# Two-layer graph convolution: the second layer's first 16 tiles gather before the last 212 hidden rows are stored, and small last groups share gather buffers

## The chip, the cores and the metric

The kernel runs on one core of one Trainium2 chip. The metric is the device time of one execution in microseconds (us); the time before is the median of 14 runs. The core has five engines with a queue each: TensorE (PE, with its weight loads as PEld), VectorE (DVE), ScalarE (ACT), GpSimd (POOL) and SyncE (SP). Every queue runs in its order, and semaphores tie the queues together. POOL issues all gathers here, SP nearly all other transfers.

## What is computed

There are N = 12500 nodes with 128 channels and E = 200000 edges, sorted by destination. Each edge has one of 10 relations, the argmax over 10 of its attribute columns. A layer averages the source rows of each (destination, relation), applies that relation's weights, and adds a root product and a bias. Two such layers, the first with a relu, are followed by a residual and a layer norm:

```
sums = segment_sum(x[src], dst * 10 + edge_type)
mean = sums / max(count, 1)
layer(x) = einsum('nrd,rdo->no', mean, w_rel) + x @ root + bias
h   = relu(layer1(x))
out = layernorm(x + layer2(h))
```

Layer 2 gathers rows of h, so in general it needs all of h.

## The kernel before

**Tiles and groups.** The edges are cut into NT = 1563 tiles of 128. A group is G = 16 tiles; NS = 95 full groups (0 to 94, tiles 0 to 1519) are followed by the small groups that start at tiles 1520, 1528, 1536, 1544 (8, 8, 8 and 8 tiles), 1552, 1556 (4 each) and 1560 (3). Both layers run the same loop, `layer` (L532), over the groups.

**One group.** `gather` (L479) issues one indirect transfer a tile on POOL (L481): 128 rows of `x` or of the hidden table `hD`, picked by `idxE`, land in a buffer `g` of 16 tiles. Every group, a small one too, takes one of three such buffers (`RING`). `ones` (L490) makes on DVE, for each tile, a 128 x 120 matrix that has the edge's weight 1/count (`wE`) at its key (relation and offset of the destination within the tile: 10 x 12 columns) and 0 elsewhere (L496); two buffers of 16. `sums` (L500) multiplies: per tile one product g^T x oh, 128 x 120, into PSUM (L507). A full group's first product waits for all its gathers; the tiles run from last to first, and only the last product tells other engines. In the small groups each product tells by itself. PSUM holds one full group, so a group's products need DVE's adds of the group before. `add` (L519) loads the tiles' first nodes into DVE registers and adds each tile's result into the ring `circle` (L530).

**Blocks.** Nodes are finished in 29 blocks: 0 to 22 of 512 nodes, then 128 each, and block 28 of 84. `done_after` says after which tile a block is complete. Blocks 24 to 28 (from node 11904) finish among the small groups: 24 after group 94, 25 after tile 1528, 26 (nodes 12160 to 12287) after 1544, 27 (12288 to 12415) after 1556 and 28 (12416 to 12499) at the end. `projected` (L404) is a root product (L408) and ten products with the ring (L416), in two halves; ACT clears the ring after each half (L417), and DVE's later adds wait for that. `block_rows` (L428) applies bias and relu (ACT, L432) and transposes on PE (L435). In layer 1 `hidden` (L442) stores h transposed (`hT`, L447), copies the rows (ACT, L450) and stores them to `hD` (SP, L383); `block_in` (L387) loads the next block and transposes it (L400, L401). In layer 2 `final` (L453) adds the residual, normalises and stores the output.

**Order.** The queues are filled by a scheduler that keeps each engine's order by program position and readiness. In the program, group k's `ones`, gathers and products come first, then `add` of group k-1 with the blocks that it completes, then some steps of a list `todo` (L595). That list prepares edge data during layer 1: chunks of 128 tiles, one every 8 groups, each in some dozen steps (sources, types with argmax, counts with one-hot compares and PE sums, L353 to L357). Each entry has a group by which it should be done, two groups ahead of its use; the due group and the number of steps left say how many are done after each group. Among the small groups the order changes: all held adds first, `ones` one group ahead, and the add directly behind the products.

**The change of layer.** Layer 2's first gather (POOL) waits for all stores to `hD`. In layer 2, before the small groups, a flag is read by the engines (L558) that says whether a slower general path, in the `If` at L740, has to run; on these inputs it does not run.

Of the kernel before, what the change touches and what calls it, by code (L numbers as in the profile page):

```python
# [9 lines left out]
F32 = mybir.dt.float32  # L10
BF16 = mybir.dt.bfloat16
I32 = mybir.dt.int32
# [32 lines left out]
def rgcn_resnorm_kernel(ctx: ExitStack, tc: tile.TileContext, x, src, dst, attr, w_rel1, root1, b1,  # L45
# [34 lines left out]
    def done_after(k):  # L80
# [6 lines left out]
            return NT  # L87
        return min(a + n for a, n in groups if a + n >= t)

    HALF = NT * P - E  # L90
    STEP = P * N // E
    assert STEP * E == P * N and C == P and E % GT == 0 and 0 < HALF < P and NT % CT and 1 < groups[-1][1] <= G
# [27 lines left out]
    idxE = keep.tile([P, NCH * CT], I32, name="idxE")  # L120
    keyE = keep.tile([P, NCH * CT], F32, name="keyE")
    wE = keep.tile([P, NCH * CT], F32, name="wE")

    def chunk_rows(c):
        return min(CT, NT - c * CT)
# [312 lines left out]
    def spans(k):  # L438
        n = block(k)[1]
        return [(p, slice(a, b)) for p, a, b in ((P, 0, n // P), (n % P, n // P, -(-n // P))) if p and b > a]  # L440

    def hidden(k, ready, sums_of):  # L442

        xb, fT = ready
        n0, n, _ = block(k)
        a, pr = block_rows(sums_of(fT, k, 0), k, 0)
        then("SP", nc.sync.dma_start(hT[:, n0:n0 + n], a[:, :n]))  # L447
        hb = fin.tile([P, 4, C], F32, name="hb")
        for p, s in spans(k):
            nc.scalar.activation(hb[:p, s], pr[:p, s], AF.Copy)  # L450
        rows_dma(hb, hD, k, True)
# [24 lines left out]

    HELD = "clamped to a node on the chip"

    def gather(table, t0, n):  # L479
        g = gpool.tile([P, G, C], F32, name="g")  # L480
        return g, [then("POOL", nc.gpsimd.indirect_dma_start(  # L481
            out=g[:, j, :], out_offset=None, in_=table, in_offset=bass.IndirectOffsetOnAxis(
                ap=idxE[:, t0 + j:t0 + j + 1], axis=0))) for j in range(n)]

    whole = mybir.DependencyInfo(mybir.DependencyClass.Sync, mybir.DependencyReason.DATA)

    def tile_sums(zp, j):
        return zp[j // HT][:, j % HT // QB, j % QB * KW:(j % QB + 1) * KW]

    def ones(k):  # L490

        t0, n = groups[k]
        oh = dpool.tile([P, G, KW], F32, name="oh")
        for j in range(n):
            t = t0 + j
            then("DVE", nc.vector.tensor_scalar(oh[:, j, :], iotaP[:, :KW], keyE[:, t:t + 1], wE[:, t:t + 1],  # L496
                                                op0=ALU.is_equal, op1=ALU.mult))
        return oh

    def sums(table, k, oh):  # L500

        t0, n = groups[k]
        end = k >= NS
        g, gathers = gather(table, t0, n)
        zp = [ps_z.tile([P, HT // QB, YB], F32, name="zp") for _ in range(0, n, HT)]
        for j in range(n) if end else reversed(range(n)):
            m = nc.tensor.matmul(tile_sums(zp, j), g[:, j, :], oh[:, j, :], start=True, stop=True)  # L507
            then("PE", m)
            if end:
                continue  # L510
            if j < n - 1:
                tc.keep_in_program_order(m)
                continue

            for d in gathers[:j]:
                tc.add_manual_dep(m.ins, d.ins.name, whole, reason="one wait per group")
        return k, zp
# [14 lines left out]
    def layer(table, l, finish, steps, flag_too=False):  # L532
# [14 lines left out]
        for k in range(NG):  # L547
            end = k >= NS
            if k and not given and done < NBLK - 1:
                given = block_in(done, l)  # L550
            if end:

                while held:
                    add_oldest()
                if not ready:
                    ready = block_in(NBLK - 1, l)
                    if flag_too:
                        loads, (flag,) = nc.values_load_multi_w_load_instructions(  # L558
                            flag_i[0:1, 0:1], min_val=0, max_val=1, skip_runtime_bounds_check_because=HELD)
                        for ld in loads:  # L560
                            tc.keep_in_program_order(ld)
                        loaded.update(("POOL", "DVE", "PE", "ACT", "SP"))
            held.append(sums(table, k, made or ones(k)))
            made = ones(k + 1) if end and k < NG - 1 else None
# [13 lines left out]
    def chain(*gens):  # L578
        for s in gens:
            yield from s  # L580
# [14 lines left out]
    todo = []  # L595
    for c in range(1, NCH):
        s = [as_steps(sources, c + 1)] if c + 1 < NCH else []
        todo.append((c * CT // G - 2, [8 + L // DB + 2], chain(*s, types(c), count(c))))
    layer(x, 0, hidden, todo)
    def flagged():  # L600

# [14 lines left out]
    fast.close()  # L616


    gp = ctx.enter_context(tc.tile_pool(name="gp", bufs=2))
    gps = ctx.enter_context(tc.tile_pool(name="gps", bufs=1, space=PSUM))  # L620

# [153 lines left out]
```

## Time and profile before

| quantity | value |
|---|---|
| median of 14 runs | 4688.63 us (4676.69 to 4694.55) |
| profiled execution | 4688.05 us, its span 4686.3 us |
| POOL busy | 2956.3 us, 63% (3126 gathers of 0.945 us) |
| DVE busy | 1909.6 us, 41% |
| PE busy | 1868.6 us, 40% |
| ACT busy | 323.6 us, 7% |
| full groups 1 to 94 of layer 1, up to tile 1520 | 84.3 to 2314.1 us |
| small groups of layer 1 and change of layer | 2314.1 to 2411.6 us |
| full groups of layer 2 | 2411.6 to 4585.4 us |
| small groups of layer 2 and end | 4585.4 to 4686.3 us |
| granted TensorE clock | 0.667 mean |

The timeline gives for each instruction its start, its duration, the engine, the line, what it writes and reads, and in brackets how long the engine had been idle before it and what ended that idle time. "remote" and "another core or an unknown queue" stand where no releaser is found; there is only one core here. "issue" means that the engine waited for nothing that the profile shows. PE's ends are modelled from the size of an instruction, so a product's result can come later than its row says. An fp32 product is two passes, so it appears twice in the count of L507.

### The profile page before, as it was taken

The numbers are of one execution on the slowest core, as the hardware profiler recorded it, in microseconds if no ns is written. First come the engines' busy times: TensorE is split into PE (matmuls) and PEld (weight loads), VectorE is DVE, ScalarE is ACT, GpSimd is POOL, SyncE is SP. The second block draws the span as 40 slices with busy tenths as digits, with TensorE's granted clock in tenths as the row PEclk, the third lists the DMA queues.
The fourth block names the chain that finished last, engine by engine and source line by source line (L and its number), as shares of the span: only waits on it lengthen the run. The fifth ranks groups of instructions, "written<-read, shape, count | busy, mean of one in ns | idle before, by whom it ended". The sixth has DMA issues, their size and how long they took to land.

```text
span 4686.3 us, 32313 instructions
## 1 busy us (share of the span) xinstructions
PE 1868.6 (40%) x8122; PEld 1447.8 (31%) x8122; DVE 1909.6 (41%) x7125; ACT 323.6 (7%) x325; POOL 2956.3 (63%) x3136
## 2 busy tenths in 40 slices
PE   2444433344443444444532433433343343334335
PEld 1333322233232332322432333322233233223224
DVE  4344444343444434444423333333333333333344
ACT  1000010000100001000110100000000000000001
POOL 6566666666656666566656666666666666666664
PEclk7666666666666666666665766666666666666667
DMA  4222222122221222211211221222222122211221
GB/s 136 60 66 77 65 67 79 50 78 62 67 78 50 79 62 67 59 50 52 54 52 45 53 60 53 53 57 55 54 53 60 53 54 57 55 51 52 56 56 43
DMA packets 177383, 284.67 MB, mean 61 GB/s; under 512 B 57799, under 2 KB 118159, under 8 KB 174063
## 3 DMA queue, kind: packets, MB, share of 16 engines
q0 software_dynamic: 100032, 205.07, 16.6%
q1 hardware_dynamic: 73967, 77.43, 5.2%
q10 hardware_dynamic: 3190, 0.02, 0.1%
q8 instruction: 69, 1.13, 0.1%
q14 instruction: 125, 1.02, 0.1%
HBM read 262.29 MB, written 20.00 MB: 60 GB/s over the span
## 4 chain that ended last, share of the span: by engine, by line
another core or an unknown queue 39%; DVE 19%; issue 15%; PE 8%; ACT 1%; DVEq 1%; ACTq 1%
DVE acc L530 10%; DVE oh L496 7%; PE zp L507 4%; PE pp L416 2%; PE pp L408 1%; DVEq L524 1%; ACT acc L417 1%; ACTq L450 1%; DVE o L472 0%; DVE st L465 0%; PE pf L355 0%; DVE v L462 0%; ACT a L432 0%; PE pf L357 0%
## 5 line engine op out<-in xcount | busy, mean ns | idle before, releaser
L507 PE MATMUL zp<-oh,g 128*128 128x120 f32 x6252 | 1212.3, 371 | 2174.3 <-issue 1935.3
L481 POOL DMA_INDIRECT g<-in_x_dram,idxE x1563 | 1478.2, 946 | 906.1 <-issue 439.9
L481 POOL DMA_INDIRECT g<-hD,idxE x1563 | 1476.8, 945 | 795.6 <-issue 444.6
L507 PEld LDWEIGHTS zp<-oh,g 128*128 128x128 f32 x6252 | 1136.6, 279 | 2321.7 <-issue 2128.5
L530 DVE TENSOR_TENSOR acc<-acc,zp 128x120 f32 x3126 | 837.9, 268 | 2367.0 <-remote 1705.1
L496 DVE TENSOR_SCALAR oh<-bank,keyE,wE 128x120 f32<-128x120 f32 x3126 | 1196.7, 393 | 12.7 <-PE zp L507 7.0
L416 PE MATMUL pp<-acc,w 128*128 128x512 f32 (+2 forms) x1160 | 451.4, 548 | 28.4 <-DVE acc L530 19.8
L417 ACT ACTIVATE acc<-zero 128x2560 f32<-128x2560 f32 (+2 forms) x116 | 228.1, 1994 | 2539.0 <-remote 1777.0
L416 PEld LDWEIGHTS pp<-acc,w 128*128 128x128 f32 x1160 | 214.1, 208 | 231.7 <-issue 203.0
L355 PE MATMUL pf<-eqb,identb 128*128 128x512 bf16 (+2 forms) x130 | 64.7, 498 | 200.2 <-DVE eqb L353 144.6
L408 PE MATMUL pp<-fT,root 128*128 128x512 f32 (+1 forms) x112 | 76.3, 774 | 94.7 <-ACT fT L401 89.6
L353 DVE TENSOR_TENSOR eqb<-pf,kh 128x1344 bf16<-128x1344 f32 (+2 forms) x65 | 100.1, 1548 | 11.8 <-issue 7.6
L462 DVE TENSOR_TENSOR v<-pf,xb 128x512 f32<-128x512 f32 (+1 forms) x28 | 17.4, 620 | 202.5 <-remote 168.8
L357 PEld LDWEIGHTS <-identb 128*128 128x128 bf16 (+2 forms) x130 | 15.9, 122 | 224.0 <-issue 219.2
L412 ACT ACTIVATE acc<-zero 128x120 f32<-128x120 f32 x24 | 7.3, 302 | 1069.4 <-DVE acc L411 474.4
L400 PE MATMUL pf<-ident,xb 128*128 128x128 f32 x97 | 24.5, 394 | 117.5 <-ACT hb L450 105.6
L435 PE MATMUL pf<-ident,a 128*128 128x128 f32 x196 | 43.3, 352 | 60.1 <-ACT a L432 52.5
L357 PE MATMUL pf<-eqb,identb 128*128 128x512 bf16 (+2 forms) x130 | 65.7, 505 | 0.0
L408 PEld LDWEIGHTS pp<-fT,root 128*128 128x128 f32 x112 | 24.0, 262 | 101.8 <-ACT fT L401 95.5
L400 PEld LDWEIGHTS pf<-ident,xb 128*128 128x128 f32 x97 | 17.9, 210 | 120.5 <-ACT hb L450 107.6
L435 PEld LDWEIGHTS pf<-ident,a 128*128 128x128 f32 x196 | 32.2, 187 | 67.4 <-ACT a L432 58.6
L169 DVE CAST idxE<-pf 128x128 int32<-128x128 f32 (+1 forms) x13 | 3.7, 282 | 85.1 <-PE pf L168 67.7
(89 smaller groups left out, 384.3 us busy)
## 6 DMA issues: line engine op xcount, KB each, us to landing
m<-in_edge_attr_dram SPq DMA_DIRECT2D x24, 1344.0 KB
g<-in_x_dram,idxE POOLq DMA_INDIRECT x1563
g<-hD,idxE POOLq DMA_INDIRECT x1563
xb<-in_x_dram SPq DMA_DIRECT2D x46, 256.0 KB
hT<-a SPq DMA_DIRECT2D x23, 256.0 KB
hD<-hb SPq DMA_DIRECT2D x23, 256.0 KB
fT<-hT SPq DMA_DIRECT2D x23, 256.0 KB
out_dram<-o SPq DMA_DIRECT2D x23, 256.0 KB
```

Source lines behind the costliest of these rows:

```text
L353: nc.vector.tensor_tensor(eq[:p], kp[:p, None, :R].to_broadcast([p, DB, R]), fore, op=ALU.is_equal)
L355: nc.tensor.matmul(pc[:p], identb[:p, :p], eq[:p, k:k + 4, L:], start=(d + k == 1), stop=False)
L357: nc.tensor.matmul(pc[:p], identb[:p, :p], back, start=False, stop=(d + k + 3 == L))
L408: nc.tensor.matmul(po[:, :n], rsb[l], fT[:, :n], start=True, stop=False)
L416: nc.tensor.matmul(po[:, :n], wsb[l][:, r, :], circle[:, r, o:o + n], start=False, stop=(r == NREL - 1))
L417: nc.scalar.activation(circle[:, q:q + H, o:o + n], zero[:, None, :n].to_broadcast([P, H, n]), AF.Copy)
L435: nc.tensor.transpose(pr[:h, t, :], a[:, t * P:t * P + h], ident)
L450: nc.scalar.activation(hb[:p, s], pr[:p, s], AF.Copy)
L481: return g, [then("POOL", nc.gpsimd.indirect_dma_start(out=g[:, j, :], out_offset=None, in_=table, in_offset=bass.IndirectOffsetOnAxis(ap= ...
L496: then("DVE", nc.vector.tensor_scalar(oh[:, j, :], iotaP[:, :KW], keyE[:, t:t + 1], wE[:, t:t + 1], op0=ALU.is_equal, op1=ALU.mult))
L507: m = nc.tensor.matmul(tile_sums(zp, j), g[:, j, :], oh[:, j, :], start=True, stop=True)
L530: nc.vector.tensor_tensor(s, s, z, op=ALU.add)
```

## The change

It has three parts.

First, EARLY = 12288 is the first node of block 27. Layer 2's group 0 gathers from `hD[:12288]` only, with indices clamped to 12287 (`idxH`) and with weights set to 0 where the source is a later node (`wH`). So it depends on the stores of blocks 0 to 26. The part of the later nodes, 128 and 84 rows, comes by products: `late_h` keeps these rows in SBUF when `hidden` makes them, and `late_w` is a matrix of weights from late node to (tile, key). `late_sums` adds two products of 480 columns for each of four PSUM banks, in front of the group's 16 products, which now accumulate.

Second, `head`, a new last entry of `todo` due by group 94, makes `idxH`, `wH` and `late_w` in one setup step and four steps of four tiles. For each tile DVE makes three one-hot matrices (`oh`, and `of` for either late block), and PE multiplies each `of` with `oh`; ACT copies the results out. The last chunk's entry is due at 90 instead of 94, since `late_w` takes the buffers of its attributes.

Third, `gather` takes a new buffer only when the tile number is a multiple of 16, so the groups 1520 and 1528 share one, as do 1536 and 1544, and 1552, 1556 and 1560.

```
+    EARLY = starts[NBLK - 2]
...
+        i = k - (NBLK - 2)
+        hb = late_h[:, i:i + 1] if i >= 0 and not anew else fin.tile([P, 4, C], F32, name="hb")
...
+    def is_head(table, t0):
+        return table is hD and t0 < G
+
+    def head():
+        nc.vector.tensor_scalar(idxH, idxE[:, :G], EARLY - 1, None, op0=ALU.min)
+        off = keep.tile([P, 2, G], F32, name="offH")
+        nc.vector.tensor_copy(off[:, 0], idxE[:, :G])
+        nc.vector.tensor_scalar(wH, off[:, 0], float(EARLY) - 0.5, None, op0=ALU.is_lt)
+        nc.vector.tensor_tensor(wH, wH, wE[:, :G], op=ALU.mult)
+        for i in (1, 0):
+            nc.vector.tensor_scalar(off[:, i], off[:, 0], -float(starts[NBLK - 2 + i]), None, op0=ALU.add)
+        late_w.extend(prep.tile([P, P // 2 * D], F32, name=f"m{i}") for i in range(2))
+        yield
+        for b in range(0, G, QB):
+            pm = [ps_f.tile([P, YB], F32, name="pf") for _ in range(2)]
+            for j in range(QB):
+                t = b + j
+                oh = prep.tile([P, KW], F32, name="ohH")
+                nc.vector.tensor_scalar(oh, iotaP[:, :KW], keyE[:, t:t + 1], wE[:, t:t + 1],
+                                        op0=ALU.is_equal, op1=ALU.mult)
+                for i in range(2):
+                    of = prep.tile([P, P], F32, name=f"of{i}")
+                    nc.vector.tensor_scalar(of, iotaP[:, :P], off[:, i, t:t + 1], None, op0=ALU.is_equal)
+                    nc.tensor.matmul(pm[i][:, j * KW:(j + 1) * KW], of, oh, start=True, stop=True)
+            for i in range(2):
+                nc.scalar.activation(late_w[i][:, b * KW:(b + QB) * KW], pm[i][:, :QB * KW], AF.Copy)
+            yield
+
     def gather(table, t0, n):
-        g = gpool.tile([P, G, C], F32, name="g")
+        o = t0 % G
+        if not o:
+            shared["g"] = gpool.tile([P, G, C], F32, name="g")
+        g = shared["g"][:, o:o + n]
+        ix = idxE
+        if is_head(table, t0):
+            table, ix = table[:EARLY, :], idxH
...
+    def late_sums(table, t0, banks):
+        if is_head(table, t0):
+            for b, z in enumerate(banks):
+                for i in range(2):
+                    n = block(NBLK - 2 + i)[1]
+                    nc.tensor.matmul(z[:, :QB * KW], late_h[:n, i, :], late_w[i][:n, b * QB * KW:(b + 1) * QB * KW],
+                                     start=(i == 0), stop=False)
...
+        late_sums(table, t0, [zp[b // 2][:, b % 2] for b in range(G // QB)] if n == G else ())
         for j in range(n) if end else reversed(range(n)):
-            m = nc.tensor.matmul(tile_sums(zp, j), g[:, j, :], oh[:, j, :], start=True, stop=True)
+            m = nc.tensor.matmul(tile_sums(zp, j), g[:, j, :], oh[:, j, :],
+                                 start=not is_head(table, t0), stop=not is_head(table, t0) or j % QB == 0)
...
-        todo.append((c * CT // G - 2, [8 + L // DB + 2], chain(*s, types(c), count(c))))
+        todo.append((c * CT // G - (2 if s else 6), [8 + L // DB + 2], chain(*s, types(c), count(c))))
+    todo.append((NS - 1, [G // QB + 1], head()))
```

More of the change, by code (lines that the diff above doesn't have):

```diff
@@ L122, in rgcn_resnorm_kernel @@
     wE = keep.tile([P, NCH * CT], F32, name="wE")
+    late_w = []
+    idxH = keep.tile([P, G], I32, name="idxH")
+    wH = keep.tile([P, G], F32, name="wH")
+    late_h = keep.tile([P, 2, C], F32, name="late_h")
     def chunk_rows(c):
@@ L440, in spans @@
         return [(p, slice(a, b)) for p, a, b in ((P, 0, n // P), (n % P, n // P, -(-n // P))) if p and b > a]
+    anew = []
     def hidden(k, ready, sums_of):
@@ L447, in hidden @@
         then("SP", nc.sync.dma_start(hT[:, n0:n0 + n], a[:, :n]))
-        hb = fin.tile([P, 4, C], F32, name="hb")
+        i = k - (NBLK - 2)
+        hb = late_h[:, i:i + 1] if i >= 0 and not anew else fin.tile([P, 4, C], F32, name="hb")
         for p, s in spans(k):
@@ L477, in rgcn_resnorm_kernel @@
     HELD = "clamped to a node on the chip"
-    def gather(table, t0, n):
-        g = gpool.tile([P, G, C], F32, name="g")
+    shared = {}
+    def is_head(table, t0):
[24 more added lines that the diff above has]
+            yield
+    def gather(table, t0, n):
+        o = t0 % G
[5 more added lines that the diff above has]
+            table, ix = table[:EARLY, :], idxH
         return g, [then("POOL", nc.gpsimd.indirect_dma_start(
             out=g[:, j, :], out_offset=None, in_=table, in_offset=bass.IndirectOffsetOnAxis(
-                ap=idxE[:, t0 + j:t0 + j + 1], axis=0))) for j in range(n)]
+                ap=ix[:, t0 + j:t0 + j + 1], axis=0))) for j in range(n)]
     whole = mybir.DependencyInfo(mybir.DependencyClass.Sync, mybir.DependencyReason.DATA)
@@ L488, in tile_sums, with ones @@
         return zp[j // HT][:, j % HT // QB, j % QB * KW:(j % QB + 1) * KW]
-    def ones(k):
+    def ones(k, table):
         t0, n = groups[k]
         oh = dpool.tile([P, G, KW], F32, name="oh")
+        w = wH if is_head(table, t0) else wE
         for j in range(n):
             t = t0 + j
-            then("DVE", nc.vector.tensor_scalar(oh[:, j, :], iotaP[:, :KW], keyE[:, t:t + 1], wE[:, t:t + 1],
+            then("DVE", nc.vector.tensor_scalar(oh[:, j, :], iotaP[:, :KW], keyE[:, t:t + 1], w[:, t:t + 1],
                                                 op0=ALU.is_equal, op1=ALU.mult))
         return oh
+    def late_sums(table, t0, banks):
[5 more added lines that the diff above has]
+                                     start=(i == 0), stop=False)
     def sums(table, k, oh):
@@ L562, in layer @@
                         loaded.update(("POOL", "DVE", "PE", "ACT", "SP"))
-            held.append(sums(table, k, made or ones(k)))
-            made = ones(k + 1) if end and k < NG - 1 else None
+            held.append(sums(table, k, made or ones(k, table)))
+            made = ones(k + 1, table) if end and k < NG - 1 else None
             if end or len(held) > 1:
@@ L616, in rgcn_resnorm_kernel @@
     fast.close()
+    anew.append(True)
     gp = ctx.enter_context(tc.tile_pool(name="gp", bufs=2))
```

## The prediction

> **What bounds the kernel now.** I read the page first, then the POOL, PE, DVE and ACT timelines around the change of layer and at the end, because the page is a mean over stages.
>
> ```profile
> PE 1868.6 (40%) x8122; PEld 1447.8 (31%) x8122; DVE 1909.6 (41%) x7125; ACT 323.6 (7%) x325; POOL 2956.3 (63%) x3136
> ...
> another core or an unknown queue 39%; DVE 19%; issue 15%; PE 8%; ACT 1%; DVEq 1%; ACTq 1%
> ```
>
> POOL is the busiest engine, and the largest share of the chain of waits has no named releaser. The POOL timeline shows the rhythm: one gather each 1.25 us (0.94 and a 0.30 gap), so a group of 16 is a run of 19.7 us, and then POOL waits for a buffer. These are the starts of layer 2's groups 0, 3 and 4.
>
> ```profile
> 2411.61 0.94 POOL L481 DMA_INDIRECT g<-hD,idxE  x1 [25.38 <-PE pp L408]
> ...
> 2479.10 0.94 POOL L481 DMA_INDIRECT g<-hD,idxE  x1 [7.84 <-remote]
> ...
> 2501.91 0.94 POOL L481 DMA_INDIRECT g<-hD,idxE  x1 [3.15 <-remote]
> ```
>
> The change of layer costs 25.38 us. Later groups start 22.8 us apart, a run of 19.7 and a wait of 3.1. What is that wait? PE and DVE of the same stretch:
>
> ```profile
> 2433.03 6.02 PE L507 MATMUL zp<-oh,g 128*128 128x120 f32 x32 [22.40 <-DMA g<-hD,idxE]
> 2482.81 3.74 PE L507 MATMUL zp<-oh,g 128*128 128x120 f32 x16 [43.77 <-DVE acc L530]
> ...
> 2478.93 0.28 DVE L530 TENSOR_TENSOR acc<-acc,zp 128x120 f32 x1 [66.53 <-remote]
> ...
> 2501.68 0.28 DVE L530 TENSOR_TENSOR acc<-acc,zp 128x120 f32 x1 [14.65 <-remote]
> ```
>
> Group 0's 32 passes (two per product) are entered at 2433.03 to 2439.05, yet DVE's add, which waits only for them, starts at 2478.93: 7.7 us after POOL's run of 48 gathers ended (2471.26). Group 1 repeats it: PE by 2489.8, DVE at 2501.68, 2.9 us after POOL's run ended at 2498.8. DVE itself was quiet from 2487.0. So I read: **while POOL issues gathers and DVE and ACT are quiet, PE's results come at a crawl**, (2478.9 - 2433.0) / 32 = 1.43 us a pass, where they are entered at 0.19. ACT's clearing of the ring, half a block after each five products, tests it on one shape:
>
> ```profile
> 4636.38 0.74 ACT L417 ACTIVATE acc<-zero 128x640 f32<-128x640 f32 x1 [10.86 <-PE pp L416]
> 4642.73 0.74 ACT L417 ACTIVATE acc<-zero 128x640 f32<-128x640 f32 x1 [5.62 <-remote]
> ...
> 4658.63 0.74 ACT L417 ACTIVATE acc<-zero 128x640 f32<-128x640 f32 x1 [9.52 <-PE pp L416]
> 4660.36 0.74 ACT L417 ACTIVATE acc<-zero 128x640 f32<-128x640 f32 x1 [0.99 <-PE pp L416]
> ```
>
> The same five products take 6.35 us under a run (4630.68 to 4645.4; DVE quiet from 4637.7) and 1.73 without. The cause of the crawl is not in the trace; I use it as found. [...]
>
> Last, the end of layer 1 (tiles 1520 on), where each small group takes a buffer of its own:
>
> ```profile
> 2325.75 0.94 POOL L481 DMA_INDIRECT g<-in_x_dram,idxE  x1 [1.88 <-remote]
> ...
> 2341.67 0.95 POOL L481 DMA_INDIRECT g<-in_x_dram,idxE  x1 [6.23 <-PE zp L507]
> ...
> 2354.75 4.59 PE L416 MATMUL pp<-acc,w 128*128 128x128 f32 x20 [6.89 <-DVE oh L496]
> ...
> 2363.62 1.51 ACT L417 ACTIVATE acc<-zero 128x640 f32<-128x640 f32 x2 [18.08 <-remote]
> ...
> 2391.05 0.32 SPq L383 DMA_DIRECT2D hD<-hb  x1
> ...
> 2409.04 0.33 SPq L383 DMA_DIRECT2D hD<-hb  x1
> ```
>
> POOL waits between short runs, and in these waits PE gets through. The last two lines are the stores of block 26 and of the last 84 nodes; layer 2's first gather follows the last store by 2.57 us.
>
> **The change, part by part.** Times are against the profiled execution: 4688.05 us, span 4686.3 and 1.75 around it; the median of 14 runs is 0.6 above.
>
> *Early gathers.* Group 0 of layer 2 needs block 26 (rows below 12288), not blocks 27 and 28. The stores lie 2409.04 - 2391.05 = 18.0 us apart, so its 16 gathers may move 18.0 earlier, and group 1 (20.0 after group 0) still finds the last rows landed. They pass nothing on POOL's queue; SP's stores are the same. Alone: -18.0.
>
> *Shared buffers, layer 1's end.* Tiles 1520 to 1535 become one run, 2314.08 to 2333.8, without the wait at 2325.75. But that wait let group 93's products finish (DVE had them at 2325.51). Now DVE falls quiet at about 2322 with some 12 passes left: 12 x 1.43 = 17 us, or the run's end and 2.9, so 2336.7, the ordinary rhythm: +11.2. Run B (1536 to 1551) is 2336.9 to 2356.6. Behind group 93 on PE stand block 22's projection (8.8 us), then through ACT its four transposes (about 4 at the crawl), then group 94's 32 passes, of which most stay until the run ends: about 2363, where now it is 2341.4: +21.6. DVE's adds, the six projections left and ACT queue behind it. From there to the last store the trace has 67.6 us; of these 10.2 are crawl (DVE's 5.58 us wait at 2351.61, where PE needed 1.9: 3.7; ACT at 2363.62, not 2357.1: 6.5). The last run (11 gathers, 2363.3 to 2377.0) covers fewer of them; I charge 3. Last store: 2363 + 67.6 - 10.2 + 3 = 2423.4, +14.4. Bounds: 0 (group 94 as now) and +21.6 (nothing of the crawl saved).
>
> *Sum at the change of layer.* Group 0 at 2391.05 + 14.4 + 2.57 = 2408.0, its run to 2427.7; last rows landed at 2426.0, about 1 later if the early run slows the last blocks (DVE has the next factors to make there, so little). Group 1 at 2428.6, now 2431.6: -3. Group 0 then has 8 more products of 480 columns, 16 passes at 0.43 (the 512-column rows at L416 step so) = 6.9 us if all lie after the run, 0 if they fit in it; I take 3. So 0 in all, bounds -18 and +12.
>
> *Making the late factors.* 48 DVE one-hots at 0.39 = 18.8 us, 32 products of 64 passes (13 us at 0.2), 8 ACT copies at 0.6, in four steps over layer 1's last groups. DVE is quiet 14.65 us per group, so the work itself is covered. The tiles of0, of1 and ohH have one buffer each: DVE waits for PE four times a step, and main adds stand behind it in DVE's order; POOL waits for those. Nearest rows: layer 1's groups with a finished block, three round trips between PE and ACT, start 26.8 us apart (group 88) against 22.8: +4 a step. Part of this wait falls under busy DVE, so +2.5 a step, +10. Below nothing: starts 20.0 apart occur where DVE stays busy, -2.8 a step, -11; above: 16 passes crawling, 23 us a step less the 11.4 that PE now loses under a run, +46. The last chunk's steps come earlier, four a group instead of two, onto the quiet 14.65 us: 0, bounds -3 and +8.
>
> *Shared buffers, layer 2's end.* Group 92 done 4585.1; run A to 4605.1 without the break at 4596.99; group 93 at 4607.8 (now 4596.7); group 94 between 4622 and 4632 (now 4608.5), as ACT's and DVE's final steps keep PE going or not: +19. Less the crawl now in the rest (6.35 - 1.73 = 4.6 at 4642.73; 3.7 at L462, 4647.83 after products of 4643.78), plus 3: +14 at the end. Bounds -8 and +21.
>
> Sum: 0 + 10 + 0 + 14 = +24: 4688.05 + 24 = **4712**.
>
> **Rivals.** *No price for long runs (faster).* If PE keeps pace in a run of 16 in the last groups, as it did at 4604.35 to 4608.5 under a run of 8, both ends stay where they are and the 18.0 is kept: 4670 with the factors at 0. It decides if group 93's products are done by about 2327 in the new trace. Against it: every full group of layer 2.
> *The factors stall layer 1.* If each wait of DVE for PE makes DVE quiet and PE crawls, a step costs about 9 (group 84's 30.1 against 22.8 is 7.3, the dearest late one): 4 x 6.5 more, 4738.
> *The early gathers still wait for the last rows,* if that wait is on all stores of hD: group 0 at 2426.0, group 1 at 2446.0, +14.4 instead of -3: 4729.
> *The ends cancel:* early gathers and factors as above, group 94 half as late at both ends: about 4712 - 7 - 10, or 4695, and 4688 with free factors.
>
> **How the numbers follow.** Two results within 0.2% (9.4 us) can't be told apart here. Forecast (4699 to 4725) 0.40, stalled factors 0.17, no early start 0.07: slower 0.64. Ends cancel 0.14: same. Free long runs 0.22: faster. The likeliest is 4712, own range 4699 to 4725. For 8 in 10: down to 4668, which takes in 4670 with 2 to spare and leaves 0.1 below; up to 4750, the stalled factors and half their bound.
>
> **What would show it.** Early start right: layer 2's first gather starts while the products of block 27 or 28 still run, and POOL's 25.38 us idle shrinks. Shared buffers as said: POOL's last runs are 16, 16 and 11, and DVE's first add of group 93 comes 2 to 3 us after the first of them ends; ACT's L417 and DVE's first adds say "remote" there. Factors: starts of groups 89 to 94 above 25. The forecast falls if the end groups' products are seen promptly inside the runs, or if the scheduler gives DVE other work there, which by the rows above would keep PE going.

## The result, and the profile after

The changed kernel takes 4734.25 us (median of 6 runs, 4726.69 to 4739.91) against 4688.63 before (28 runs): 1.0099 times as long, 95% interval 1.0089 to 1.0109. It is 45.6 us slower; the forecast was 23, at 4712 us. The measured time lies above the forecast's own range (4699 to 4725) and inside its wider one (4668 to 4750). The kernel before itself took 3950 us in one of the four later comparisons and 4685 to 4728 in the other three (3950 and 4686 on one and the same chip), so every kernel below is compared only with runs of the kernel before that were made beside it, and the two conditions are named by their rhythm in layer 2, groups 20.0 us apart or groups 22.7 to 23.0 apart.

The page of the changed kernel, its busy times and then the engines' shares of the chain of waits:

```profile
PE 1895.0 (40%) x8202; PEld 1467.6 (31%) x8202; DVE 1927.4 (41%) x7179; ACT 328.0 (7%) x333; POOL 2953.6 (62%) x3136
...
another core or an unknown queue 28%; DVE 14%; issue 6%; PE 2%; DVEq 1%; ACT 0%; DMA 0%; ACTq 0%
```

The work added is small (PE 26 us more, DVE 18), and POOL does the same gathers. So the loss must be in waits. POOL's timeline of the changed kernel shows where: the start of tile 1520 in layer 1, the next gather that waited, layer 2's groups 0 and 1, and then layer 2's tiles 1520, 1536 and 1552.

```profile
2310.72 0.94 POOL L529 DMA_INDIRECT g<-in_x_dram,idxE  x1 [3.26 <-remote]
...
2379.43 0.94 POOL L529 DMA_INDIRECT g<-in_x_dram,idxE  x1 [29.09 <-PE zp L566]
...
2424.02 0.94 POOL L529 DMA_INDIRECT g<-hD,idxH  x1 [31.16 <-DMA hD<-hb]
...
2451.04 0.94 POOL L529 DMA_INDIRECT g<-hD,idxE  x1 [7.36 <-PE pp L415]
...
4601.98 0.94 POOL L529 DMA_INDIRECT g<-hD,idxE  x1 [3.12 <-remote]
...
4624.69 0.94 POOL L529 DMA_INDIRECT g<-hD,idxE  x1 [3.04 <-remote]
...
4646.85 0.94 POOL L529 DMA_INDIRECT g<-hD,idxE  x1 [2.50 <-remote]
```

Tile 1520 of layer 1 starts 3.4 us earlier than before (2310.72, was 2314.08). Then 32 gathers run without a stop, where POOL waited twice before (at 2325.75 and 2341.67), and POOL stands 29.09 us for group 94. Layer 2's first gather is 12.4 us later than before (2424.02, was 2411.61), group 1 is 19.4 later (2451.04, was 2431.6), tile 1520 of layer 2 is 16.6 later (4601.98, was 4585.38). From there to the end it takes 125.3 us (4727.3 - 4601.98) where it took 100.9. So: -3 before tile 1520, some +20 at the end of layer 1 and the change of layer, +24 at the end of layer 2.

What POOL waited for at 2379.43 stands in DVE's, PE's and SP's rows of the same stretch:

```profile
2318.78 8.76 PE L423 MATMUL pp<-acc,w 128*128 128x512 f32 x20
...
2324.85 0.91 DVE L590 TENSOR_TENSOR acc<-acc,zp 128x120 f32 x3 [8.92 <-remote]
...
2358.65 1.12 PE L442 MATMUL pf<-ident,a 128*128 128x128 f32 x4 [31.12 <-ACT a L439]
...
2359.56 0.62 PE L515 MATMUL pf<-ohH,of 128*128 128x120 f32 x2
...
2361.33 0.40 DVE L510 TENSOR_SCALAR ohH<-bank,keyE,wE 128x120 f32<-128x120 f32 x1 [35.57 <-PE pf L515]
...
2372.38 6.78 PE L566 MATMUL zp<-oh,g 128*128 128x120 f32 x32 [3.33 <-DVE acc L590]
...
2421.55 0.32 SPq L390 DMA_DIRECT2D hD<-hb  x1
...
2448.81 0.33 SPq L390 DMA_DIRECT2D hD<-late_h  x1
```

Read it from the DVE row at 2361.33. DVE stood 35.57 us in front of a one-hot of the last factor step (L510), because the buffer was still held by a product (L515) that stands on PE behind block 22's projection (L423) and transposes (L442). The projection was entered by 2327.5, but PE's transposes waited 31.12 us for ACT, which waited for the projection to be seen (ACT cleared the ring's first half at 2343.76, the second at 2355.69); POOL's run of gathers ended at 2350.34. DVE's later adds and one-hots stand behind that wait, and PE's products of group 94 need such adds ([3.33 <-DVE acc L590]), so they start at 2372.38. The two stores show that the early start itself works: the first gather is 2.47 us behind block 26's store (2421.55), and does not wait for the last store (2448.81).

At the end of layer 2 POOL's runs are 16, 16 and 11 gathers (the last three of POOL's rows above). DVE's adds of group 93 start 2.8 us behind the first of them, and block 23 is seen later still:

```profile
4624.46 4.98 DVE L590 TENSOR_TENSOR acc<-acc,zp 128x120 f32 x16 [14.62 <-remote]
...
4633.29 1.84 PE L423 MATMUL pp<-acc,w 128*128 128x128 f32 x15
...
4655.89 0.74 ACT L424 ACTIVATE acc<-zero 128x640 f32<-128x640 f32 x1 [26.18 <-remote]
...
4662.95 0.74 ACT L424 ACTIVATE acc<-zero 128x640 f32<-128x640 f32 x1 [6.14 <-remote]
```

Block 23's projection is entered from 4633.29 on; its first half is answered by ACT at 4655.89, its second at 4662.95. POOL is through with all gathers at 4660.34, only 1.7 us later than before, but by then five blocks are still to be projected, one after the other.

### The profile page after: what moved, and what is told of

Its sections match the earlier page's. It is cut to its first block, busy times and chain, and to the rows that moved or that the text cites. A ratio compares the mean times of both kernels' runs of the same rounds, so it can differ in the third digit from the quotient of the medians.

```text
span 4727.3 us, 32531 instructions
## 1 busy us (share of the span) xinstructions
PE 1895.0 (40%) x8202; PEld 1467.6 (31%) x8202; DVE 1927.4 (41%) x7179; ACT 328.0 (7%) x333; POOL 2953.6 (62%) x3136
## 4 chain that ended last, share of the span: by engine, by line
another core or an unknown queue 28%; DVE 14%; issue 6%; PE 2%; DVEq 1%; ACT 0%; DMA 0%; ACTq 0%
DVE acc L590 7%; DVE oh L545 5%; PE zp L566 1%; PE pp L423 1%; DVEq L584 1%; DVE o L482 0%; DVE st L475 0%; ACT acc L424 0%; DVE v L472 0%; DVE mv L476 0%; DVEq L590 0%; DVE rstd L479 0%; PE pf L442 0%; PE pf L515 0%
## 5 line engine op out<-in xcount | busy, mean ns | idle before, releaser
L529 POOL DMA_INDIRECT g<-hD,idxE x1547 | 1460.3, 944 | 756.4 <-issue 446.1
L590 DVE TENSOR_TENSOR acc<-acc,zp 128x120 f32 x3126 | 837.6, 268 | 2274.8 <-remote 1660.9
L423 PE MATMUL pp<-acc,w 128*128 128x512 f32 (+2 forms) x1160 | 450.2, 547 | 25.2 <-DVE acc L590 15.7
L423 PEld LDWEIGHTS pp<-acc,w 128*128 128x128 f32 x1160 | 214.2, 208 | 228.7 <-issue 203.7
L360 DVE TENSOR_TENSOR eqb<-pf,kh 128x1344 bf16<-128x1344 f32 (+2 forms) x65 | 100.1, 1548 | 21.6 <-issue 19.3
L442 PE MATMUL pf<-ident,a 128*128 128x128 f32 x196 | 43.5, 353 | 118.5 <-ACT a L439 114.9
L407 PE MATMUL pf<-ident,xb 128*128 128x128 f32 x97 | 24.4, 392 | 119.3 <-ACT hb L460 106.7
L442 PEld LDWEIGHTS pf<-ident,a 128*128 128x128 f32 x196 | 31.9, 186 | 126.5 <-ACT a L439 121.7
L407 PEld LDWEIGHTS pf<-ident,xb 128*128 128x128 f32 x97 | 17.8, 209 | 122.2 <-ACT hb L460 108.7
```

The lines of the kernel that those rows point to most:

```text
L360: nc.vector.tensor_tensor(eq[:p], kp[:p, None, :R].to_broadcast([p, DB, R]), fore, op=ALU.is_equal)
L423: nc.tensor.matmul(po[:, :n], wsb[l][:, r, :], circle[:, r, o:o + n], start=False, stop=(r == NREL - 1))
L442: nc.tensor.transpose(pr[:h, t, :], a[:, t * P:t * P + h], ident)
L529: return g, [then("POOL", nc.gpsimd.indirect_dma_start(out=g[:, j, :], out_offset=None, in_=table, in_offset=bass.IndirectOffsetOnAxis(ap= ...
L590: nc.vector.tensor_tensor(s, s, z, op=ALU.add)
```

## The experiments

My theory going in was the forecast's: the shared buffers make long runs of gathers, PE's products come late under a run, and so both ends lose. The rivals were that the factors cost the end of layer 1, and that the cause of late products is another than quiet engines. Spans below are of the profiled runs, cut at POOL's rows; "mid" is layer 2's first gather to its tile 1520.

| kernel | ratio to before (95%) | layer 1, groups 88 to 94 | tile 1520 to layer 2's first gather | mid | tile 1520 to end |
|---|---|---|---|---|---|
| before | 1 | 165.7 | 97.5 | 2173.8 | 100.9 |
| changed | 1.0099 (1.0089 to 1.0109) | 166.8 | 113.3 | 2178.0 | 125.3 |
| changed, again | 1.0082 (1.0069 to 1.0095) | 171.7 | 114.8 | 2196.6 | 112.7 |
| own buffers, second run | 0.9999 (0.9990 to 1.0008) | 171.1 | 89.4 | 2194.4 | 100.3 |
| factors alone | 1.0027 (1.0018 to 1.0036) | 169.8 | 107.2 | 2189.9 | 101.3 |
| factors earlier | 1.0019 (1.0010 to 1.0028) | 206.6 | 76.4 | 2180.0 | 99.2 |
| factors buffered | 0.9976 (0.9965 to 0.9987) | 159.7 | 82.0 | 2183.0 | 99.0 |
| paused | 1.0035 (1.0023 to 1.0047) | 167.3 | 87.4 | 2177.0 | 117.3 |

Rows three to five come from one comparison on one chip (groups 23.0 apart), the others from chips with groups 22.7 to 22.8 apart. "Layer 1, groups 88 to 94" is from the start of group 88 to tile 1520.

### Own buffers and shared buffers alone, with groups 20.0 us apart

Own buffers: the changed kernel, but every small group takes a buffer.

```
-        o = t0 % G
-        if not o:
-            shared["g"] = gpool.tile([P, G, C], F32, name="g")
-        g = shared["g"][:, o:o + n]
+        g = gpool.tile([P, G, C], F32, name="g")
```

> The changed kernel, with a buffer of its own for every small group again; early gathers, late factors and late products stay. Theory (the long runs of the shared buffers cost both ends): the 24.4 us that the end of layer 2 lost (tile 1520 to the end: 125.3 us in the changed kernel, 100.9 before) come back, and so do the some 20 us that the stretch from tile 1520 of layer 1 to layer 2's steady groups lost: 4685 to 4692 us. If the early start then shows its 18.0 us as well, down to 4670. Rival (the last step of the factors, whose products stand on PE in front of group 94's, costs the end of layer 1): only layer 2's end comes back, 4734 - 24 = 4710 us.

Shared buffers alone is the opposite edit, made to the kernel before.

> The kernel before, with shared buffers for the small groups as the only edit: no early gathers, no factors. Theory (the shared buffers cost both ends): layer 2's end costs 24 us, layer 1's end 14 to 20: 4727 to 4733 us, POOL's last runs 16, 16 and 11 in both layers. Rival (the factors cost layer 1's end): layer 2's end alone, 4688 + 24 = 4712 us. Rival (the long runs are free): 4688 us.

This comparison met a kernel before of 3950.15 us. Own buffers took 3936.29, ratio 0.9967 (0.9954 to 0.9979); shared buffers alone 3950.38, ratio 1.0000 (0.9991 to 1.0009). None of the expected times could come, but the pair says more than they would have. In the profile of shared buffers alone the group of layer 2's gathers (busy time and mean, then idle time ahead of them by what ended it):

```profile
L486 POOL DMA_INDIRECT g<-hD,idxE x1563 | 1474.9, 944 | 495.3 <-issue 467.8 <-PE pp L408 19.3 <-DMA g<-hD,idxE 7.6
```

the list of its transfers, with the time from issue to landing:

```profile
g<-hD,idxE POOLq DMA_INDIRECT x1563, 2.5
```

and in its timeline one group's products and the first add:

```profile
2058.76 5.83 PE L512 MATMUL zp<-oh,g 128*128 128x120 f32 x32 [14.42 <-DMA g<-hD,idxE]
...
2064.62 0.28 DVE L535 TENSOR_TENSOR acc<-acc,zp 128x120 f32 x1 [12.16 <-PE zp L512]
```

Within layer 2 POOL does not stop for the groups' products: 467.8 of its 495.3 us are issue, and the 19.3 for L408 have the label of the wait at the change of layer. PE's 32 passes end at 2064.59, and DVE adds at 2064.62, in the middle of an unbroken run of gathers. So here products are seen at once under a run (within 1.2 us of the last pass in all 58 groups that can be followed), and here shared buffers cost nothing (ratio 1.0000). That is the forecast's first rival, "no price for long runs", in the condition that it asked for. The early start, with its factors, is worth 13.9 us of the 18.0. The changed kernel itself was not run in this condition.

### Idle copies on ACT or DVE

The forecast's reading said that products are late only while DVE and ACT are quiet. So the kernel before was given something to do there: copies to a scratch tile.

```
+        if not end:
+            nc.scalar.activation(junk[:, :8], g[:, n - 1, :8], AF.Copy)
+            for _ in range(16):
+                nc.scalar.activation(junk, zero, AF.Copy)
```

> The kernel before, with 16 idle copies of 128 x 512 on ACT after each full group's gathers have landed (some 10 us a group, they write to a scratch tile), in both layers. Theory (products come at a crawl only while POOL issues and both DVE and ACT are quiet): the products of a group are out well before POOL's run ends, POOL no longer waits 3.1 us a group, groups start 20.0 apart: 94 x 2.8 = 263 us less in layer 2 and some 100 to 250 in layer 1: 4200 to 4450 us, less what ACT's clearing of the ring loses behind the copies. Rival (the results wait for a pause of POOL whatever the other engines do, or only DVE's work helps): groups stay 22.8 apart, 4688 us or some 50 more, since the copies stand before the clearing.

```
+            if not end:
+                for _ in range(24):
+                    tc.keep_in_program_order(nc.vector.tensor_copy(junk[:, :W], columns))
```

> The kernel before, with 24 idle copies of 128 x 128 on DVE a full group (some 5 to 8 us, a scratch tile), spread over its adds and one-hots, in both layers. Theory (quiet DVE lets PE crawl): groups start between 20.0 and 21.5 apart in layer 2, 100 to 260 us less there, the whole 4300 to 4600 us. Rival (the results wait for a pause of POOL): groups stay 22.8 apart or come later by the time that the copies stand in front of adds, 4688 to 4900 us.

Both ran with groups 20.0 apart, where nothing is late, and only cost: ACT's copies 1.0678 (1.0662 to 1.0694), since each block's clearing stands behind them and groups with a finished block start 22 to 31 us apart; DVE's copies 1.0121 (1.0105 to 1.0136). So the DVE version was run once more.

> The kernel before with 24 idle copies of 128 x 128 on DVE a full group, once more, since the first time it ran where groups are 20.0 us apart without it (there 1.0121). On a chip with groups 22.8 to 23.0 apart: theory (results come late only while DVE and ACT are quiet), groups 20.0 to 21.5 apart and 0.85 to 0.94 of the kernel before; rival (the results wait for a pause of POOL, whatever DVE does), groups 22.8 or more apart and 1.00 to 1.04.

This time the groups were 22.9 apart without and with the copies: 1.0128 (1.0110 to 1.0146), the same cost as where nothing is late. One group of layer 2 in its profile, PE, then DVE and POOL:

```profile
3011.87 6.50 PE L508 MATMUL zp<-oh,g 128*128 128x120 f32 x32 [4.77 <-issue]
...
3026.10 0.23 DVE L570 COPY junk<-columns 128x128 f32<-128x128 f32 x1 [1.19 <-DVE junk L570]
...
3026.18 0.96 POOL L482 DMA_INDIRECT g<-hD,idxE  x1 [0.30 <-issue]
...
3029.67 0.28 DVE L531 TENSOR_TENSOR acc<-acc,zp 128x120 f32 x1 [3.34 <-remote]
...
3029.90 0.95 POOL L482 DMA_INDIRECT g<-hD,idxE  x1 [2.76 <-remote]
```

The passes were entered by 3018.4 and DVE worked until 3026.3, yet the first add came at 3029.67, 2.5 us after the last gather of POOL's run had ended at 3027.1. Of 49 groups of layer 2 that can be followed (passes that start between 2600 and 4400 us and stand in the trace without a gap of 1.5 us) 46 are seen 2.4 to 3.3 us after the end of a run, by DVE or by POOL, whichever goes on first; in about half of them DVE's own first add comes up to 5 us later, behind its copies. DVE's work does not bring products forward. That condition of my theory falls, and the rival, that results wait for a pause of POOL, takes its place.

The two runs of this one program show something else. Here are the idle copies in the page of the first (groups 20.0 apart) and in the list of lines of the second (busy time and mean, then DVE's idle time ahead of them by what ended it):

```profile
L570 DVE COPY junk<-columns 128x128 f32<-128x128 f32 x4560 | 1104.9, 242 | 9.9
...
L570 DVE COPY junk<-columns 128x128 f32<-128x128 f32 x4560 | 1094.9, 240 | 789.4 <-remote 347.5 <-DVE oh L497 303.6 <-DVE acc L531 52.6
```

Ahead of the same 4560 copies DVE stood 9.9 us in the one condition and 789.4 us in the other, 303.6 of them for its own one-hots. So in the slow rhythm DVE sees even its own results late, and it is not PE's results alone that come late.

### The parts apart, with groups 23.0 us apart

> The changed kernel as it is, beside the kernel before on one chip. The chip of the last comparison ran the kernel before in 3950 us, with groups 20.0 us apart and products seen at once; the chip of the first profiles ran it in 4688, with groups 22.8 apart. Theory (the changed kernel's loss is the late results under long runs of gathers): where groups are 20.0 apart the loss is gone and the early start is left, 0.996 to 0.998 of the kernel before, as with own buffers; where they are 22.8 apart, 1.009 to 1.011. Rival (factors or late products cost time by themselves): slower than own buffers by 5 us or more also where groups are 20.0 apart.

> The changed kernel with a buffer of its own for every small group, beside the changed kernel on the same chip. Theory: where groups are 20.0 us apart the same as the changed kernel within 5 us, 0.996 to 0.998 of the kernel before; where they are 22.8 apart 35 to 45 us less than the changed kernel, 4685 to 4700 us. Rival (the last step of the factors costs the end of layer 1): there only 24 us less, 4710.

Factors alone is own buffers with one line changed, so that the factors are made but layer 2's group 0 gathers all rows as before:

```
     def is_head(table, t0):
-        return table is hD and t0 < G
+        return False
```

> The changed kernel with own buffers, and the factors made but not used: layer 2's group 0 gathers as before from all of the hidden table, with no late products. Theory (POOL sets the time where groups are 20.0 apart, and the factors fit beside it): 1.000 within 0.1% of the kernel before there, so the early start alone is worth the 14 us between this and own buffers. Where groups are 22.8 apart: 0 to +10 us by the forecast's term, 4689 to 4699. Rival (the factors' last step stands in front of group 94's products): +10 to +20 us on either chip.

The kernel before took 4727.54 here. Changed 4765.10, own buffers 4727.56, factors alone 4741.49: shared buffers +37.5, factors +14 (by the ratio, +8.5 to +17), early start with its late products -13.9. Each is the difference of two neighbours in one chain of edits, so they add up to the whole by construction; each part was measured on top of the ones before it. Shared buffers without the factors were not run where groups are 23.0 apart. The shared buffers cost both ends, as my theory said (25.4 us at layer 1's end, 12.4 at layer 2's, by the table), and not 24 in all, as the rival said. Own buffers come back to 1.000 and no further, because the factors eat the early start. The factors' +14 lies in the range that the rival gave them (+10 to +20) and above mine (0 to +10), though the interval reaches into mine. The rows of POOL, own buffers first:

```profile
2378.79 0.95 POOL L526 DMA_INDIRECT g<-in_x_dram,idxE  x1 [18.00 <-PE zp L563]
...
2428.78 0.94 POOL L526 DMA_INDIRECT g<-hD,idxH  x1 [7.72 <-DMA hD<-hb]
...
2455.76 0.95 POOL L526 DMA_INDIRECT g<-hD,idxE  x1 [7.28 <-DMA hD<-late_h]
```

and factors alone, whose tile 1520 starts at 2336.41 (own buffers: 2339.42):

```profile
2443.59 0.95 POOL L526 DMA_INDIRECT g<-hD,idxE  x1 [25.32 <-PE pp L415]
```

From tile 1520 to the first gather it is 89.4 us with the early start and 107.2 without: 17.8. But group 1 then waits 7.28 us for the last rows, 27.0 after group 0 instead of 20.0, and layer 2's first five groups take 117.8 us instead of 113.6. So 4.2 of the 17.8 are given back at once. The factors show in the 18.00 us for which POOL waits at 2378.79: tiles 1520 to 1535 take 39.4 us, and 27.6 in the kernel before, where POOL's wait at the same place is 6.23. DVE's row in front of the last factor step, with own buffers:

```profile
2361.79 0.40 DVE L510 TENSOR_SCALAR ohH<-bank,keyE,wE 128x120 f32<-128x120 f32 x1 [10.02 <-issue]
```

This is the place at which DVE stood 35.57 us in the changed kernel, and 31.46 in its second profile (at 2389.47). With own buffers it stands 10.02, with the factors alone 10.18. So most of the long wait belongs to the two edits together: the factors put DVE behind PE, and the shared buffers' long run keeps it there.

### Where the factors' cost lies

Two edits tell the place on PE's queue from the waits in DVE's. In the first the factors are due three groups earlier, so that none of their products stands in front of group 94's:

```
-        todo.append((c * CT // G - (2 if s else 6), [8 + L // DB + 2], chain(*s, types(c), count(c))))
-    todo.append((NS - 1, [G // QB + 1], head()))
+        todo.append((c * CT // G - 2 - 3 * max(0, c + 3 - NCH), [8 + L // DB + 2], chain(*s, types(c), count(c))))
+    todo.append((NS - 4, [G // QB + 1], head()))
```

> Own buffers, early gathers, and the factors three groups earlier (due by group 91; the last two chunks of edge data are due 3 and 6 groups earlier, to make room), so that the last factor products no longer stand on PE between block 22's projection and group 94's products. Theory (of the factors' 14 us on the chip with groups 23 apart, the some 10 that show between tile 1520 and layer 2's first gather are this place in PE's order): there 10 us less than with own buffers alone, 0.9975 to 0.9990 of the kernel before, tile 1520 of layer 1 to the first gather some 80 us where own buffers alone had 89.4. On a chip with groups 20.0 apart as own buffers, 0.9967. Rival (the cost is DVE's waits for PE in each step, wherever they stand): 1.000 where groups are 23 apart.

1.0019 (1.0010 to 1.0028). The stretch from tile 1520 to the first gather did fall, to 76.4, as the theory had it (80). But the groups before took 206.6 us instead of some 170, so the whole is above both expectations. A pair of rows shows the larger piece, DVE and POOL in group 92 (55.3 us long, 30.5 with own buffers):

```profile
2269.40 0.40 DVE L510 TENSOR_SCALAR ohH<-bank,keyE,wE 128x120 f32<-128x120 f32 x1 [35.19 <-PE pf L515]
...
2294.03 0.95 POOL L526 DMA_INDIRECT g<-in_x_dram,idxE  x1 [35.58 <-PE pf L515]
```

The wait moved with the factors, and it grew from own buffers' 10.02 us to 35.19: here, as in the changed kernel, POOL has 32 gathers to issue without a stop (2218.72 to 2258.45) while DVE waits. The other piece, some 14 us in group 88, is not the factors': the steps of edge data, which this edit moves too, stand there, and no factor product does. So the place in front of group 94's products is not the cause by itself; DVE's round trip to PE is, which in both places fell behind a block's projection and lasted until 11 us after the end of POOL's run (2269.40 against 2258.45 here, 2361.33 against 2350.34 in the changed kernel). Half of each theory stands. In the second edit each of a step's four tiles has one-hot buffers of its own, and DVE waits once a step:

```
-                oh = prep.tile([P, KW], F32, name="ohH")
+                oh = prep.tile([P, KW], F32, name=f"ohH{j}")
...
-                    of = prep.tile([P, P], F32, name=f"of{i}")
+                    of = prep.tile([P, P], F32, name=f"of{i}{j}")
```

> Own buffers, early gathers, factors at their place of the change, but with four buffers for each of the factors' one-hot tiles, so that DVE waits for PE once a step and not four times. Theory (the factors' 14 us come from DVE's round trips to PE inside a step, each of which lasts to POOL's next pause where groups are 22.8 to 23.0 apart): there 5 to 12 us less than own buffers alone, 0.997 to 0.999 of the kernel before. Rival (the cost is the last step's place on PE, in front of group 94's products): 1.000, and tile 1520 to the first gather still some 89 us. Where groups are 20.0 apart: 0.9967, as own buffers alone.

4673.34 against 4684.67 us: 0.9976 (0.9965 to 0.9987), inside the expected 0.997 to 0.999 and against the rival's 1.000. The factor products of the last step, and POOL's rows of tile 1520, 1536 and the first early gather:

```profile
2304.42 1.05 POOL L526 DMA_INDIRECT g<-in_x_dram,idxE  x1 [3.23 <-remote]
...
2326.03 3.61 PE L515 MATMUL pf<-ohH,of 128*128 128x120 f32 x16
...
2336.82 0.95 POOL L526 DMA_INDIRECT g<-in_x_dram,idxE  x1 [11.06 <-PE zp L563]
...
2386.44 0.95 POOL L526 DMA_INDIRECT g<-hD,idxH  x1 [7.42 <-DMA hD<-hb]
```

All 16 passes go in one piece, none of the factors' one-hots waits for L515 any more, and groups 88 to 94 take 159.7 us. This version is faster than the kernel before, and by its ratio about 1% faster than the changed one; it has own buffers too, and the comparison that tells the factors' share is the one with own buffers' 0.9999, taken on another chip.

### Pauses put in on purpose

If results are seen only when POOL pauses between gathers, then idle work on POOL should make the changed kernel faster. 13 iotas to a scratch tile (`pause`) stand in front of each small group that shares a buffer, eight times in all.

```
+        if o:
+            pause()
```

> The changed kernel, shared buffers included, with some 3 us of idle work on POOL (13 iotas to a scratch tile) in front of each small group that shares a buffer (tiles 1528, 1544, 1556 and 1560, in both layers): 24 us more work for POOL. Theory (products are seen only when POOL pauses between gathers, so what the shared buffers took away is the pauses): where groups are 22.8 to 23.0 apart it is faster than the changed kernel by 15 to 35 us, 1.000 to 1.006 of the kernel before. Rival (results are late because DVE and ACT are quiet, or long runs are free and the loss is elsewhere): slower than the changed kernel by up to 24 us, 1.010 to 1.015. Where groups are 20.0 apart: 10 to 24 us over own buffers' 0.9967, 0.999 to 1.003.

1.0035 (1.0023 to 1.0047), inside the theory's 1.000 to 1.006 and well below the changed kernel's 1.0082 to 1.0099, although POOL has eight pauses of 2.7 us more to go through. At layer 1's end it regains all (87.4 us, changed 113.3 and 114.8, own buffers 89.4), and DVE's wait in front of the last factor step is 10.20 us (at 2339.76), as with own buffers. At layer 2's end it does not (117.3). Its rows there, POOL's pauses and DVE:

```profile
4591.31 2.52 POOL L399 IOTA rest<- 128x128 f32 x13
...
4593.06 4.99 DVE L610 TENSOR_TENSOR acc<-acc,zp 128x120 f32 x16 [3.56 <-PE zp L586]
...
4613.69 2.51 POOL L399 IOTA rest<- 128x128 f32 x13
...
4617.34 0.69 DVE L490 TENSOR_TENSOR v<-pf,xb 128x512 f32<-128x512 f32 x1 [19.30 <-remote]
```

Group 93's adds start inside the first pause. The next hand-over that DVE needs, block 22's transposed rows, comes 1 us behind the next pause, 24 us later. In these rows the chain of hand-overs moves about one link a pause, and here the pauses are still 22 us apart; the kernel before has one more of them in this stretch. That this is the whole of what stays lost at layer 2's end is argued, not shown.

The last run puts the same pause into the middle of every full group of the kernel before.

```
+            if j == HT:
+                pause()
```

> The kernel before with the same 3 us of idle work on POOL in the middle of each of the 190 full groups, 570 us more work for POOL. Theory (products are seen only when POOL pauses): where groups are 22.8 to 23.0 apart the wait at the end of a group goes, because the products were seen in the middle pause, and groups stay 22.7 to 23.5 apart: 0.99 to 1.03 of the kernel before. Rival (a group's wait has another cause): the pauses add up, groups 25.5 to 26 apart, 1.10 to 1.13. Where groups are 20.0 apart: 23 apart, 1.13 to 1.15.

1.0170 (1.0127 to 1.0213): about 97 us more, for 190 pauses that each keep POOL from gathering 2.4 us longer than the usual gap, 456 us in all. Two of its pauses in layer 2:

```profile
3031.50 2.53 POOL L392 IOTA rest<- 128x128 f32 x13
...
3033.16 0.28 DVE L553 TENSOR_TENSOR acc<-acc,zp 128x120 f32 x1 [2.48 <-PE zp L530]
...
3034.18 0.96 POOL L503 DMA_INDIRECT g<-hD,idxE  x1 [0.16 <-issue]
...
3053.91 2.53 POOL L392 IOTA rest<- 128x128 f32 x13
...
3053.96 0.28 DVE L553 TENSOR_TENSOR acc<-acc,zp 128x120 f32 x1 [12.71 <-remote]
...
3056.60 0.96 POOL L503 DMA_INDIRECT g<-hD,idxE  x1 [0.16 <-issue]
```

The first adds moved from the end of a group into the pause in its middle, and the wait at the group's end is gone: 3034.18 to 3056.60 is 22.4 us, 16 gathers and one pause, where the kernel before has 16 gathers and a wait of 3.1. The pauses do not add up, they replace each other; a wait that had nothing to do with POOL's pauses would have stayed. The theory is not exact, though: of 55 groups that can be followed 13 are seen at once (none in the kernel before), but 30 inside a run, nearly all of them up to 8 us behind a pause. A pause of 2.7 us is about as long as the 2.5 to 3.1 that the kernel before needs, and a run delays results without quite stopping them. The 97 us are in the groups with a finished block (24 to 37 us apart); that their hand-overs need more than the one pause is argued, not shown.

## Why the prediction was right or wrong

**The reading of the bound.** That products and whatever follows them are late under POOL's runs, and that a wait of 2.5 to 3 us after each run is the price, was right where groups are 22.8 apart, and decides the case. The condition "while DVE and ACT are quiet" was wrong (DVE's copies: still 22.9). Whether the passes themselves crawl, at the 1.43 us a pass that I worked out, or only the news of them waits, is not settled, but more speaks for news. In the kernel before 60 of 64 groups are seen 2.5 to 3.1 us behind a run, though their last passes had been entered anything from 9 to 13 us before they were seen; and DVE, which has no passes, waits 303.6 us for its own one-hots ahead of its idle copies. Against it, ACT's first clear of block 22 in the changed kernel came at 2343.76, inside the run of 32, so results are not held back altogether. In the sums both put the results 2 to 3 us behind a run, which is why a half-wrong reading still gave the sign.

**Early gathers alone, -18.0.** Measured 17.8 (107.2 to 89.4). Right.

**The change of layer.** For group 1 I had 20.6 us behind group 0, with 1 us for last blocks that the early run slows, and 3 us for the late products. Measured 27.0: the store of block 26 and the last store, 18.0 us apart before, are 27.3 apart (27.2 with own buffers). So this term was 9 us and not 1. By group 5 own buffers have won back 2.8 of the 7.0 lost at group 1, so a cost of the late products does not show. That 4.2 us of the 17.8 go back in all, where I had 4, is luck.

**Shared buffers, layer 1's end, +14.4 with bounds 0 and +21.6.** Measured 25.4 us beside own buffers (114.8 and 89.4): outside my bound. The step that failed is group 93 seen at "2336.7, the ordinary rhythm", and with it the runs of 16, 16 and 11. DVE's first three adds of group 93 came at 2324.85, inside the run and 6 us behind the last of its passes; so no pause followed the first 16 gathers, and POOL ran 32 and then stopped for 29 us. Behind those three adds DVE stood 35.57 us in front of the factors (10.02 with own buffers), which holds group 94 back. I had priced the shared buffers and the factors side by side; in the same stretch one lengthens the other.

**Making the late factors, +10 with bounds -11 and +46.** Measured +8.5 to +17. The mechanism is the one named, one buffer a tile and DVE waiting for PE with the adds behind it, as the run with four buffers shows. The spread over four steps at 2.5 each was wrong: of groups 89 to 94 only one started late (30.2 us after the group before, 25.2 before the change), and tile 1520 even came earlier. DVE's waits of 6 to 12 us in the earlier steps delay POOL at most in that one group. The larger cost sits in the last step, which meets a block's projection (11.8 us in tiles 1520 to 1535, with own buffers). "Starts of groups 89 to 94 above 25" was a poor sign to look for.

**Shared buffers, layer 2's end, +14.** 24.4 in the first pair of profiles (changed and before), 12.4 in the second (changed and own buffers). The runs and the adds of group 93 came as forecast; what it costs depends on whether block 23's answer catches a pause (ACT at 4695.82 in the second profile, 22.9 us after the second run began; at 4655.89 in the first, 31.2 us after). Bounds of -8 and +21 were a little narrow.

**The sum, +24.** 37.5 and 45.6 measured. The sign and the causes hold. By parts, in the second comparison: shared buffers 37.5 (forecast 28.4), factors 14 (10), early gathers with late products -13.9 (-14.4). Most of what is missing is at layer 1's end; in the first pair of profiles layer 2's end adds 10 more.

**The rivals.** "No price for long runs" is true where groups are 20.0 apart, and only there (1.0000 for shared buffers alone): the add comes 0.03 us behind the products in that condition, and 11 us behind them in the other (3029.67 against 3018.4 with the idle copies on DVE). "The early gathers still wait for the last rows" is out: 2.47 us behind block 26's store. "The ends cancel" is out. "The factors stall layer 1" had the right wait and the wrong price: the changed kernel has waits of 6 to 12 us in the earlier steps, which cost one group 5 us, and one of 35 us in the last.

## What to carry to other kernels

Count hand-overs between engines, not only busy time: here a tile with one buffer made its writer wait for the reader, 10 us for a one-hot of 0.4 where a block's projection stood in front of the reader on PE's queue, and 35 where a long run of gathers fell on it too; with four buffers no one-hot waited for L515. The merge here removed waits, and with them moments in which other engines were served (37.5 us slower where groups are 23.0 apart); look at what happened in such waits before calling them idle. And take the same kernel's time in more than one comparison: an edit worth -0.3% here was worth nothing there, and one that cost 0.8% there was free here.

## What the runs showed of the hardware that was not expected

The kernel before took 3950 us or 4685 to 4728 us, and both 3950 and 4686 on one chip. Its profile is of the slow rhythm; in the quick one, shared buffers alone stand for it, with the same time. The gathers cost POOL the same in both profiles (944 and 945 ns each), the granted TensorE clock was 0.705 against 0.667, and a group's 32 passes were entered in 5.8 and 6.0 us. What differs is when results are seen: DVE's add comes within 1.2 us of the last pass in all 58 groups that can be followed of shared buffers alone, and 2.5 to 3.1 us after the end of POOL's run in 60 of 64 of the kernel before, where groups then start 22.8 us apart instead of 20.0. DVE's waits for its own one-hots, 303.6 us ahead of the idle copies in the slow rhythm where in the quick one all its idle time there is 9.9, show that this is not a matter of PE alone.

One trait goes along with it in the trace. The trace of shared buffers alone (groups 20.0 apart) holds 49983 landings on the gathers' semaphores, 16.0 for each of the 3126 gathers; the trace of the kernel before (22.8 apart) holds 11934, 3.8 for each, and its list of transfers has no landing time for them. All four profiles with groups 20.0 apart hold 49972 to 49992, all ten of the slow rhythm 10394 to 11934. Whether this has a part in the late results no run here shows: no kernel was run without these records, and the low count may be a result of the same cause instead. Why the slow rhythm comes and goes stays open, and so does a kernel that avoids it.
